# A four-layer image network on one core: image 0's gram matrix by transposes, weights made inside the loop, gram products of early images spread out

## The chip, the cores and the metric

The kernel runs on one NeuronCore of a Trainium2 chip. A core has four engines that compute: PE (matrix products, results in PSUM), DVE (vector work), ACT (activations and copies) and POOL. SP only issues DMAs; POOL issues some too. Each engine takes its own instructions in order and waits for others by semaphores; 16 DMA engines do the transfers. The metric is the time of one execution on the device, in microseconds (us), over three runs.

## The reference, cut to what matters

Sixteen images x of 64 channels and 128 x 128 points, in fp32, pass through four layers. Each layer is x + f(groupnorm(x)), with a norm over pairs of channels.

```
# layer 0
gram = einsum('bcn,bdn->bcd', xf, xf) / N          # xf = normed x, N = 128*128
f    = conv_w @ (gram @ xf)
# layer 1
f = |sobel_x(x)| + |sobel_y(x)|
# layer 2
f = conv3x3(temporal_shift(x), W) + b
# layer 3
y = conv1x1(conv3x3(x, w_bin), w1x1) + b1
f = clip(leaky(batchnorm(y)), 0, 255)              # batchnorm over all 16 images
```

Layer 0 needs the gram matrix of an image before anything else of that image can be computed, and the batch norm of layer 3 needs all images before anything can be written out.

## The kernel before

**What is set up.** Constants, biases and weights are loaded; the weights of layer 2 (w2, wm, pk2) and of layer 3 (w3, pk3, which are products of w_bin and w1x1, made by PE and copied by DVE) are put together at the start (lines 118 to 247). SP carries the constants, ACT's queue the weights. `consts` is one table `kc`; `k("I")`, its first 128 columns, is the identity.

**The loop.** The work is a list of steps written out by hand (line 911): 164 steps of four quarters q. Half an image, 64 rows, is 8 chunks of R = 8 rows; a tile has both halves of an image on its 128 partitions (64 channels twice). Front does layer 0's mixing and layer 1 (Sobel) for image b in the steps 15 + 8b to 22 + 8b, after a lead-in of three steps; Layer2 starts at 25 + 8b, Layer3 at 35 + 8b. Gram loads image b and makes its gram matrix ahead of Front. `InOrder` keeps each engine's instructions in the order in which this code issues them, so a place in the loop is a place in each engine's queue.

**Gram.** An image is read with its rows on partitions: eight loads `xr` of 8 channels each (three buffers), 512 KB in runs of 512 bytes, and eight ACT copies into `xw`, which holds for every row of the image its columns by channel, and a column of ones. Then 128 products `pg<-xw` (64 channels by 65) add up the gram matrix and the sums, in groups of 44, 42 and 42. `gram_chain` takes it to the mixing matrix `abd` and the coefficients `co` by small products, DVE operations and two square roots on ACT; each `yield` of it ends its turn in one quarter (`tick`). `pace` gives image b its first step and its speed: image 0 in steps 0 to 9 at one load per step and so on, with 4 steps for its chain; images 1 to 6 at double speed (2 units per quarter, four steps and a half); the later ones in eight steps and the chain. At double speed the three groups of products stand in three quarters one after the other.

**Front.** `load(i)` brings a chunk of x (two DMAs of 256 KB, two buffers). `mix(i, g)` multiplies half a chunk with `abd` into the PSUM tile `po` (one buffer); `prepare(i, g)` is ACT's normalization of it into `xh`; `sobel(i, q)` is six DVE operations, two absolute values on ACT, two more on DVE. The first of them, u<-xh with 1170 elements, starts a chunk and needs the chunk and one row of the next. At i = -3 Front also loads two edge rows (`xe`) and writes a row of zeros from `w0` to `x2_d`.

**The end.** As the last images finish, their results are read again with the layer's input, normalized and written out (lines 986 to 994).

Of the kernel before, what the change touches and what calls it, by code (L numbers as in the profile page):

```python
# [10 lines left out]
F32 = mybir.dt.float32  # L11
# [9 lines left out]
R = 8  # L21
# [23 lines left out]
def single(table, n):  # L45

    for o in range(2):
        planes = [i for m, i, half, _ in table if (m, half) == (n, o)]
        if len(planes) == 1:
            return o, planes[0]  # L50
# [58 lines left out]
def tile_kernel(ctx: ExitStack, tc: tile.TileContext, x, cw_h, w2_t, b2, wbin_t, w1_t, b1, gamma, beta, consts, out):  # L109
# [6 lines left out]
    small = ctx.enter_context(tc.tile_pool(name="small", bufs=4))  # L116

    kc = cpool.tile([P, K_END], F32, name="kc")
    nc.sync.dma_start(kc, consts)

    def k(name):
        return kc[:, AT[name][0]:AT[name][1]]

    def load_const(src, shape, name):
        t = cpool.tile(shape, F32, name=name)
        nc.sync.dma_start(t, src)
        return t

    cwh = load_const(cw_h, [P, C], "cwh")
    b2_sb = load_const(b2, [P, 1], "b2_sb")  # L130
    b1_sb = load_const(b1, [P, 1], "b1_sb")
    gamma_sb = load_const(gamma, [P, 1], "gamma_sb")
    beta_sb = load_const(beta, [P, 1], "beta_sb")
    bn_sum = cpool.tile([P, B * NS], F32, name="bn_sum")
    bn_sq = cpool.tile([P, B * NS], F32, name="bn_sq")

# [5 lines left out]
    def flat(ap):  # L142
        return ap.rearrange("p j w -> p (j w)")

    def halves(d, h, r0, n):

        v = d[0:C * HW].rearrange("(c r) -> c r", r=HW)
        return v[:, (h * HH + r0) * W:(h * HH + r0 + n) * W]
# [20 lines left out]
    def sv(name, n=1):  # L169
        return small.tile([P, n], F32, tag=name, name=name)  # L170

    def cols(o):
        return slice(o * C, (o + 1) * C)
# [13 lines left out]
    def sm(n, rows=P):  # L187
        if n > 8:
            return bank[0:rows, P:P + n]
        turn[0] = (turn[0] + 1) % 16  # L190
        return bank[0:rows, 8 * turn[0]:8 * turn[0] + n]
# [1 line left out]


    xw = wpool.tile([P, W // 2, C + 1, 2], F32, name="xw")
    nc.gpsimd.memset(xw[:, :, C, :], 1.0)

    xh = wpool.tile([P, 3, R + 2, W + 2], F32, name="xh")
    nc.gpsimd.memset(xh, 0.0)
    junk = wpool.tile([P, R * W], mybir.dt.bfloat16, name="junk")  # L200
    wbd = wpool.tile([P, P], F32, name="wbd")
    nc.gpsimd.memset(wbd, 0.0)

    w2 = wpool.tile([P, 3, 3, P], F32, name="w2")
    w3 = wpool.tile([P, 3, 3, P], F32, name="w3")
    nc.gpsimd.memset(w2, 0.0)
    nc.gpsimd.memset(w3, 0.0)
    for slot, i, o, ky in TO_SLOTS:
        nc.scalar.dma_start(w2[i * C:(i + 1) * C, slot, :, o * C:(o + 1) * C], w2_t[:, ky])

    wm = wpool.tile([P, 3, P], F32, name="wm")
    for n in range(2):
        o = 1 - single(TO_SLOTS, n)[0]
        nc.vector.tensor_copy(wm[:, :, cols(o)], w2[:, n, :, cols(o)])
    w0 = wpool.tile([P, P], F32, name="w0")
    nc.gpsimd.memset(w0, 0.0)

    wb = work.tile([P, R + 1, W + 2], F32, tag="u", name="wb")
    wb = flat(wb)[0:C, 0:9 * C].rearrange("p (y x c) -> p y x c", y=3, x=3)
    w1 = work.tile([P, R, W + 2], F32, tag="e", name="w1", bufs=1)[0:C, 0, 0:C]  # L220
    nc.scalar.dma_start(wb, wbin_t)
    nc.scalar.dma_start(w1, w1_t)
    for ky in range(3):
        pw = sm(3 * C, rows=C).rearrange("p (k c) -> p k c", k=3)
        for kx in range(3):
            nc.tensor.matmul(pw[:, kx, :], wb[:, ky, kx, :], w1, start=True, stop=True)
        for slot, i, o, kk in TO_PAIRS:
            if kk == ky:
                nc.vector.tensor_copy(w3[i * C:(i + 1) * C, slot, :, o * C:(o + 1) * C], pw)

    packed = {}
    for name, w, table in (("pk2", w2, TO_SLOTS), ("pk3", w3, TO_PAIRS)):
        nc.vector.tensor_add(w[:, 2], w[:, 0], w[:, 1])
        packed[name] = wpool.tile([P, 2, C], F32, name=name)
        for n in range(2):
            o, i = single(table, n)
            for kx, half in ((1, i), (0, 1 - i)):
                nc.vector.tensor_copy(
                    packed[name][half * C:(half + 1) * C, n], w[i * C:(i + 1) * C, n, kx, o * C:(o + 1) * C]
                )  # L240

    diffs, twins = {}, {}
    for name in ("d2", "d3"):
        diffs[name] = wpool.tile([P, 2, CP, W + 2], F32, name=name)
        nc.gpsimd.memset(diffs[name], 0.0)
        twins[name] = wpool.tile([P, 2, CP, W + 2], F32, name=f"q{name}")
        nc.gpsimd.memset(twins[name], 0.0)


    chains = []  # L250
# [50 lines left out]
    def gram_chain(b, pg):  # L301
# [77 lines left out]
            yield  # L379
        pk = sm(1)  # L380
        small_product(pk, pp.rearrange("p s c -> p (s c)"), k("q"))
        yield
        bias = sv("bias")
        dve.tensor_copy(bias, av[:, 2:3])
        st1 = sv("st1", 2)
# [18 lines left out]
        dve.tensor_copy(co[:, 3:4], mean)  # L404
        lead[b] = abd, co

    class Gram:
        first, last = 0, NS + 1

# [2 lines left out]

        def at(self, i, q):
            b = self.b
            CG = C // 8
            if i < NS:
                if q == 0 and i != 1:
                    for m in range(i + (1 if i == 2 else 2) if i else 0, min(i + 3, NS)):
                        t = xin.tile([P, CG, W], F32, tag="xr", name=f"xr_{b}_{m}", bufs=3)
                        sp.dma_start(t, x[b].rearrange("c h w -> h c w")[:, m * CG:(m + 1) * CG, :])  # L420
                        self.xr[m] = t

                if q == 3 and i > 0:
                    for m in (0, 1) if i == 1 else (i,):
                        act.copy(
                            xw[:, :, m * CG:(m + 1) * CG, :].rearrange("p w c t -> p c w t"),
                            self.xr.pop(m).rearrange("p c (w t) -> p c w t", t=2),
                        )
                return
            n = 4 * (i - NS) + q  # L430
            if n == 0:
                self.pg = ps_g.tile([P, CP, W], F32, tag="g", name=f"pg_{b}")[:, 0, 0:C + 1]

            for _ in range({0: 44, 2: 42, 4: 42}.get(n, 0)):
                w = self.w
                s = w % 2
                pe.matmul(
                    self.pg[s * C:(s + 1) * C, :], xw[:, w // 2, 0:C, s], xw[:, w // 2, :, s],
                    start=(w < 2), stop=(w >= W - 2),
                )  # L440
                last[0] = s
                self.w += 1
            if n == 6:
                chains.append(gram_chain(b, self.pg))


    lo, hi = slice(0, C), slice(C, P)
# [2 lines left out]
    class Front:  # L450
# [17 lines left out]
            self.xs[i] = t  # L468

        def mix(self, i, g):  # L470
            po = ps_po.tile([P, CP, W], F32, tag="po", name=f"po_{self.b}_{i}_{g}")
            small_product(po, self.abd, self.xs[i][:, g * CP:(g + 1) * CP, :])
            self.po[i, g] = po

# [8 lines left out]
        def at(self, i, q):  # L483
            b = self.b
            if q == 0:
                if i == -3:

                    self.xe = xin.tile([P, W], F32, tag="xe", name=f"xe_{b}", bufs=1)
                    sp.dma_start(self.xe[lo], x[b][:, HH, :])
                    sp.dma_start(self.xe[hi], x[b][:, HH - 1, :])  # L490
                    sp.dma_start(x2_d[b][0:W].rearrange("(p w) -> p w", p=1), w0[0:1, 0:W])
                if i + 3 < NS:
                    self.load(i + 3)
                if -1 <= i < NS - 1:
                    self.prepare(i + 1, 1)
                if 1 <= i:
                    self.store(i - 1)
                    act.activation(
                        junk.rearrange("p (j w) -> p j w", w=W), self.x2.pop(i - 1), AF.Square,
                        accum_out=self.st[:, 1, i - 1:i],  # L500
                    )
                if i == NS:
                    chains.append(coefficients(self.st, lambda co: coefs2.update({b: co}), b2_sb))
# [360 lines left out]
    def run(stage, b, i, q):  # L864
        if 0 <= b < B and stage.first <= i <= stage.last:
            if (stage, b) not in live:
                live[stage, b] = stage(b)
            live[stage, b].at(i, q)


    pace = {}
    at = 0
    for b in range(B):
        half = 1 <= b <= 2 * EARLY
        pace[b] = at, 2 if half else 1

        at += (NS // 2 if half else NS) + {0: 4, 2 * EARLY: 2}.get(b, 0)
    last_one = NS * (B - 1) + starts[0][1]
    steps = last_one + NS + 1

# [27 lines left out]
            loaded.append((yt, rt))  # L908
            fetched[0] += 1

    for step in range(steps):
        for q in range(4):
            for b in range(B):

# [8 lines left out]
            if q == 3:  # L923
                for b in range(B):
                    run(Layer2, b, step - starts[1][1] - NS * b, "last of 3")
            for b in range(B):
                at, n = pace[b]
                for m in range(n):
                    v = 4 * n * (step - at) + n * q + m
                    run(Gram, b, v // 4, v % 4)  # L930
            tick()

            if step == last_one - NS and q == 0:
# [99 lines left out]
```

## Time and profile before

| | us |
|---|---|
| median of 3 runs | 2804.1 (2804.09 to 2806.65) |
| profiled execution | 2800.37 |
| its span, first to last instruction | 2798.6 |
| PE / DVE / ACT / POOL busy | 2222.1 / 2201.4 / 2120.1 / 859.5 |
| gram products of image 0 (pg<-xw x256 records) | 26.7 to 36.7 |
| first mix (po<-x,abd) | 47.25 |
| first Sobel operation (step 15) | 59.08 |
| step 47 begins | 528.97 |

The span is that of the trace of one execution; the time of that execution includes what lies around it. "Busy" adds up the time in which an engine had an instruction running; a share of the whole span averages over stages with different limits, so a stage is read by itself. In the rows of the profile, "x256" counts records: an fp32 product leaves two. The number in brackets is the idle time of that engine before the row, and what ended it. Nearly all instructions have line 73, that of the helper which keeps order; they are told apart by their tiles, written output<-inputs.

Section 2 of the page, 40 equal slices of about 70 us, gives the tenths of busy time:

```profile
PE   4568899999999999999999999999999995000000
DVE  3999999898989898989898989999997435333332
ACT  4667779888888888888888888998997667333332
PEclk7679999999999999999999999999999998555555
```

Three regimes are seen: a ramp of some seven slices, a long middle with all engines near full, and an end in which PE has nothing to do and DMA writes the output.

### The profile page before, as it was taken

The numbers are of one execution on the slowest core, as the hardware profiler recorded it, in microseconds if no ns is written. First come the engines' busy times: TensorE is split into PE (matmuls) and PEld (weight loads), VectorE is DVE, ScalarE is ACT, GpSimd is POOL, SyncE is SP. The second block draws the span as 40 slices with busy tenths as digits, with TensorE's granted clock in tenths as the row PEclk, the third lists the DMA queues.
The fourth block names the chain that finished last, engine by engine and source line by source line (L and its number), as shares of the span: only waits on it lengthen the run. The fifth ranks groups of instructions, "written<-read, shape, count | busy, mean of one in ns | idle before, by whom it ended". The sixth has DMA issues, their size and how long they took to land. (4 is left out here: it accounts for less than half of the span.)

```text
span 2798.6 us, 46299 instructions
## 1 busy us (share of the span) xinstructions
PE 2222.1 (79%) x14772; PEld 1088.8 (39%) x14772; DVE 2201.4 (79%) x3758; ACT 2120.1 (76%) x3171; POOL 859.5 (31%) x1326
## 2 busy tenths in 40 slices
PE   4568899999999999999999999999999995000000
PEld 2323444444444545353534353566666641000000
DVE  3999999898989898989898989999997435333332
ACT  4667779888888888888888888998997667333332
POOL 1035433343434343434343434444444310000000
PEclk7679999999999999999999999999999998555555
DMA  6789878888888888888888777888877767999999
GB/s 168 196 221 233 237 198 237 218 232 212 230 215 221 222 220 219 222 216 227 221 219 227 214 184 197 209 204 214 209 207 187 218 192 273 420 420 420 420 420 387
DMA packets 688880, 685.95 MB, mean 245 GB/s; under 512 B 61744, under 2 KB 590144, under 8 KB 688640
## 3 DMA queue, kind: packets, MB, share of 16 engines
q1 hardware_dynamic: 662656, 614.42, 73.9%
q0 software_dynamic: 24576, 68.12, 10.0%
q8 instruction: 119, 1.95, 0.3%
q14 instruction: 121, 0.99, 0.1%
q10 hardware_dynamic: 1408, 0.46, 0.1%
HBM read 346.23 MB, written 268.44 MB: 220 GB/s over the span
## 5 line engine op out<-in xcount | busy, mean ns | idle before, releaser
L73 PE MATMUL two<-d,w 128*64 128x508 f32 (+2 forms) x2560 | 898.2, 586 | 0.0
L73 PE MATMUL two<-d,wi 128*64 128x508 f32 (+3 forms) x1536 | 626.6, 576 | 0.0
L73 POOL DMA_DIRECT2D qd<-d x512 | 269.8, 529 | 882.2 <-issue 330.0
L73 PE MATMUL two<-qd,pk 128*64 128x512 f32 (+1 forms) x1024 | 518.5, 587 | 1.6 <-DMA qd<-d 1.1
L73 POOL TENSOR_SCALAR edges<-v,co 64x8 f32<-64x8 f32 x512 | 335.2, 655 | 352.5 <-ACT v L73 244.4
L73 PE MATMUL po<-x,abd 128*64 128x512 f32 x1024 | 386.2, 631 | 60.4 <-ACT xh L73 60.4
L73 PEld LDWEIGHTS two<-d,w 128*64 128x64 f32 x2560 | 297.9, 136 | 288.7 <-issue 221.2
L73 PE MATMUL one<-v,w 128*64 128x508 f32 (+2 forms) x1600 | 409.0, 578 | 0.0
L73 PE MATMUL one<-v,wi 128*64 128x508 f32 (+3 forms) x1536 | 407.4, 590 | 0.0
L73 DVE TENSOR_TENSOR d<-v 128x512 f32<-128x512 f32 (+1 forms) x512 | 346.1, 679 | 44.4 <-POOL v L73 17.1
L73 ACT COPY qd<-d 64x512 f32<-64x512 f32 x512 | 315.2, 616 | 21.0 <-DVE d L73 14.5
L73 ACT ACTIVATE xh<-po,co 128x128 f32<-128x128 f32 (+1 forms) x480 | 275.3, 621 | 51.0 <-PE po L73 48.7
L73 DVE SCALAR_TENSOR_TENSOR e<-e 128x1032 f32<-128x1032 f32 (+1 forms) x256 | 313.2, 1223 | 0.0
L73 DVE SCALAR_TENSOR_TENSOR y<-two,c 128x1024 f32<-128x1024 f32 x128 | 156.1, 1219 | 125.6 <-ACT v L73 72.4
L73 PEld LDWEIGHTS two<-d,wi 128*64 128x64 f32 x1536 | 196.1, 135 | 143.2 <-issue 107.7
L73 POOL TENSOR_SCALAR v<-v,kc 128x9 f32<-128x9 f32 x256 | 238.4, 944 | 11.9
L73 ACT ACTIVATE v<-x,co 128x512 f32<-128x512 f32 (+2 forms) x368 | 234.9, 704 | 0.0
L73 PEld LDWEIGHTS one<-v,w 128*64 128x64 f32 x1600 | 163.3, 137 | 177.4 <-issue 130.0
L73 PEld LDWEIGHTS one<-v,wi 128*64 128x64 f32 x1536 | 156.0, 138 | 162.6 <-issue 126.4
L73 ACT ACTIVATE u<-u 128x1024 f32<-128x1024 f32 x128 | 135.4, 1058 | 90.3 <-DVE u L73 89.9
L73 DVE SCALAR_TENSOR_TENSOR u<-xh 128x1170 f32<-128x1170 f32 x128 | 175.7, 1372 | 12.2 <-ACT xh L73 9.8
L73 PEld LDWEIGHTS po<-x,abd 128*64 128x64 f32 x1024 | 111.0, 140 | 175.4 <-ACT xh L73 92.3
(154 smaller groups left out, 3442.4 us busy)
## 6 DMA issues: line engine op xcount, KB each, us to landing
xr<-in_x SPq DMA_DIRECT2D x128, 512.0 KB, 6.7
x<-in_x SPq DMA_DIRECT2D x256, 256.0 KB, 4.0
x_d<-u SPq DMA_DIRECT2D x512, 128.0 KB, 3.6
y_d<-y SPq DMA_DIRECT2D x512, 128.0 KB, 4.0
x_d<-x SPq DMA_DIRECT2D x496, 128.0 KB, 2.5
qd<-d POOLq DMA_DIRECT2D x256, 130.0 KB, 3.0
qd<-d POOLq DMA_DIRECT2D x256, 129.8 KB, 3.6
v<-x_d SPq DMA_DIRECT2D x448, 72.1 KB, 3.0
```

Source lines behind the costliest of these rows:

```text
L73: return self.tc.keep_in_program_order(call(*args, **kwargs))
```

## The change

Four things are done.

1. Image 0 leaves the class Gram. A new function `first_gram` runs ahead of the loop: it loads image 0 by channels in eight tiles (each two DMAs of 256 KB, runs of 4 KB), transposes 128 x 128 blocks of them on PE (64 in all) into PSUM, copies the two halves into `xw` on DVE and ACT, and makes the 128 gram products chunk by chunk, those of chunk m after the transposes of chunk m + 1. It then issues Front's lead-in for image 0 with the loads of two chunks, the eight loads of image 1 for its gram, and image 0's gram chain, with five of image 1's ACT copies between its links; the other three copies come in step 15. The loop starts at step 13.
2. The loads of constants and weights go to POOL's queue, but for the identity, which is first on SP. The products that make w3 move into steps 17, 18 and 19 (their copies to ACT), the rest of the weights into step 20 (copies on POOL, two additions on DVE).
3. Images 1 to 6 keep their steps, but each quarter has one unit of its own (`half(r)`): loads at r = 3 to 10, copies at 6 to 13, the groups of products at r = 14, 16 and 18 (image 1: one later), the chain from 19.
4. Two of the first mixes of image 0 use the PSUM buffers of `two` in place of `po`.

```diff
+    sp.dma_start(kc[:, 0:P], consts[:, 0:P])
+    pool.dma_start(kc[:, P:K_END], consts[:, P:K_END])
+    for t, src in ((wb, wbin_t), (w1, w1_t), (cwh, cw_h)):
+        pool.dma_start(t, src)
...
     for slot, i, o, ky in TO_SLOTS:
-        nc.scalar.dma_start(w2[i * C:(i + 1) * C, slot, :, o * C:(o + 1) * C], w2_t[:, ky])
+        pool.dma_start(w2[i * C:(i + 1) * C, slot, :, o * C:(o + 1) * C], w2_t[:, ky])
     w0 = wpool.tile([P, P], F32, name="w0")
+    pool.memset(w0, 0.0)
...
+    def weights_of_layer_3(ky):
+        pw = bank[C:P, 512 - 3 * C:512].rearrange("p (k c) -> p k c", k=3)
+        for kx in range(3):
+            pe.matmul(pw[:, kx, :], wb[:, ky, kx, :], w1, start=True, stop=True)
+        for slot, i, o, kk in TO_PAIRS:
+            if kk == ky:
+                act.copy(w3[i * C:(i + 1) * C, slot, :, o * C:(o + 1) * C], pw)
...
+    def first_gram():
+        pg = ps_g.tile([P, CP, W], F32, tag="g", name="pg_0")[:, 0, 0:C + 1]
+        src = []
+        t = sv("sd")
+        dve.memset(t, 1.0)
+        act.activation(t, t, AF.Sqrt)
+        for m in range(NS):
+            t = ring.tile([P, 2, CP, W], F32, tag="x3", name=f"x_first_{m}", bufs=NS + 2)
+            t = t.rearrange("p a j w -> p (a j w)")
+            for h in range(2):
+                sp.dma_start(t[h * C:(h + 1) * C], halves(x[0].rearrange("c h w -> (c h w)"), h, m * R, R))
+            src.append(t)
+        for m in range(NS + 1):
+            if m < NS:
+                two = ps_two.tile([P, 2, CP, W], F32, tag="two", name=f"turned_{m}").rearrange("p a j w -> p (a j) w")
+                for j in range(R):
+                    pe.transpose(two[:, j], src[m][:, j * P:(j + 1) * P], k("I"))
+                for h, copy in ((0, dve.tensor_copy), (1, act.copy)):
+                    copy(xw[:, m * R:(m + 1) * R, 0:C, h], two[:, :, h * C:(h + 1) * C])
+            if m > 0:
+                for w in range(2 * R * (m - 1), 2 * R * m):
+                    gram_product(pg, w)
+        run(Front, 0, Front.first, 0)
+        live[Front, 0].load(1)
+        for m in range(NS):
+            t = ring.tile([P, C // 8, W], F32, tag="x3", name=f"xr_1_{m}", bufs=NS + 2)
+            sp.dma_start(t, x[1].rearrange("c h w -> h c w")[:, m * C // 8:(m + 1) * C // 8, :])
+            rows.append(t)
+        for link, _ in enumerate(gram_chain(0, pg)):
+            if link in (2, 3, 4, 5, 6):
+                rows_to_columns(1, link - 2, rows[link - 2])
...
+        def half(self, r):
+            if self.b > 1 and 6 <= r < 6 + NS:
+                rows_to_columns(self.b, r - 6, self.xr.pop(r - 6))
+            if self.b > 1 and 3 <= r < 3 + NS:
+                self.load(r - 3)
+            self.part({14: 44, 16: 42, 18: 42}.get(r - (self.b == 1), 0))
+            if r - (self.b == 1) == 19:
+                chains.append(gram_chain(self.b, self.pg))
...
         def mix(self, i, g):
-            po = ps_po.tile([P, CP, W], F32, tag="po", name=f"po_{self.b}_{i}_{g}")
+            if self.b == 0 and (i, g) in ((0, 1), (1, 0)):
+                po = ps_two.tile([P, 2, CP, W], F32, tag="two", name=f"po_0_{i}_{g}")[:, 0]
+            else:
+                po = ps_po.tile([P, CP, W], F32, tag="po", name=f"po_{self.b}_{i}_{g}")
...
-    for step in range(steps):
+    for step in range(starts[2][1] - 2, steps):
...
+            first = starts[2][1]
+            if step == first and q < 3:
+                rows_to_columns(1, NS - 3 + q, rows[NS - 3 + q])
+            if q == 1 and first + 2 <= step < first + 5:
+                weights_of_layer_3(step - first - 2)
+            if q == 1 and step == first + 5:
+                other_weights()
```

More of the change, by code (lines that the diff above doesn't have):

```diff
@@ L118, in tile_kernel, with const @@
     kc = cpool.tile([P, K_END], F32, name="kc")
-    nc.sync.dma_start(kc, consts)
     def k(name):
         return kc[:, AT[name][0]:AT[name][1]]
[L124 to L133, printed above, removed]
+    def const(shape, name):
+        return cpool.tile(shape, F32, name=name)
+    cwh = const([P, C], "cwh")
+    b2_sb, b1_sb, gamma_sb, beta_sb = (const([P, 1], n) for n in ("b2_sb", "b1_sb", "gamma_sb", "beta_sb"))
     bn_sum = cpool.tile([P, B * NS], F32, name="bn_sum")
@@ L195, in tile_kernel @@
     xw = wpool.tile([P, W // 2, C + 1, 2], F32, name="xw")
-    nc.gpsimd.memset(xw[:, :, C, :], 1.0)
-    xh = wpool.tile([P, 3, R + 2, W + 2], F32, name="xh")
-    nc.gpsimd.memset(xh, 0.0)
+    pool.memset(xw[:, :, C, :], 1.0)
+    wb = ring.tile([P, (R + 1) * W + 2], F32, tag="v2", name="wb", bufs=3)
+    wb = wb[0:C, 0:9 * C].rearrange("p (y x c) -> p y x c", y=3, x=3)
+    w1 = ring.tile([P, R + 1, W], F32, tag="v3", name="w1")[0:C, 0, 0:C]
+    sp.dma_start(kc[:, 0:P], consts[:, 0:P])
+    pool.dma_start(kc[:, P:K_END], consts[:, P:K_END])
@@ L200, in tile_kernel @@
+    for t, src in ((wb, wbin_t), (w1, w1_t), (cwh, cw_h)):
+        pool.dma_start(t, src)
     junk = wpool.tile([P, R * W], mybir.dt.bfloat16, name="junk")
     wbd = wpool.tile([P, P], F32, name="wbd")
-    nc.gpsimd.memset(wbd, 0.0)
+    pool.memset(wbd, 0.0)
     w2 = wpool.tile([P, 3, 3, P], F32, name="w2")
     w3 = wpool.tile([P, 3, 3, P], F32, name="w3")
-    nc.gpsimd.memset(w2, 0.0)
-    nc.gpsimd.memset(w3, 0.0)
-    for slot, i, o, ky in TO_SLOTS:
-        nc.scalar.dma_start(w2[i * C:(i + 1) * C, slot, :, o * C:(o + 1) * C], w2_t[:, ky])
@@ L211, in tile_kernel @@
[L211 to L214, printed above, removed]
-    w0 = wpool.tile([P, P], F32, name="w0")
[L216 to L240, printed above, removed]
+    pool.memset(w3, 0.0)
@@ L242, in tile_kernel @@
+    xh = wpool.tile([P, 3, R + 2, W + 2], F32, name="xh")
+    pool.memset(xh, 0.0)
+    pool.memset(w2, 0.0)
+    for t, src in ((b2_sb, b2), (b1_sb, b1), (gamma_sb, gamma), (beta_sb, beta)):
+        pool.dma_start(t, src)
+    for slot, i, o, ky in TO_SLOTS:
+        pool.dma_start(w2[i * C:(i + 1) * C, slot, :, o * C:(o + 1) * C], w2_t[:, ky])
+    w0 = wpool.tile([P, P], F32, name="w0")
+    pool.memset(w0, 0.0)
     diffs, twins = {}, {}
@@ L244, in tile_kernel, with other_weights @@
         diffs[name] = wpool.tile([P, 2, CP, W + 2], F32, name=name)
-        nc.gpsimd.memset(diffs[name], 0.0)
+        pool.memset(diffs[name], 0.0)
         twins[name] = wpool.tile([P, 2, CP, W + 2], F32, name=f"q{name}")
-        nc.gpsimd.memset(twins[name], 0.0)
+        pool.memset(twins[name], 0.0)
+    def weights_of_layer_3(ky):
[5 more added lines that the diff above has]
+                act.copy(w3[i * C:(i + 1) * C, slot, :, o * C:(o + 1) * C], pw)
+    wm = wpool.tile([P, 3, P], F32, name="wm")
+    packed = {}
+    def other_weights():
+        for n in range(2):
+            o = 1 - single(TO_SLOTS, n)[0]
+            pool.tensor_copy(wm[:, :, cols(o)], w2[:, n, :, cols(o)])
+        for name, w, table in (("pk2", w2, TO_SLOTS), ("pk3", w3, TO_PAIRS)):
+            dve.tensor_add(w[:, 2], w[:, 0], w[:, 1])
+            packed[name] = wpool.tile([P, 2, C], F32, name=name)
+            for n in range(2):
+                o, i = single(table, n)
+                for kx, half in ((1, i), (0, 1 - i)):
+                    pool.tensor_copy(
+                        packed[name][half * C:(half + 1) * C, n], w[i * C:(i + 1) * C, n, kx, o * C:(o + 1) * C]
+                    )
     chains = []
@@ L381, in gram_chain @@
         small_product(pk, pp.rearrange("p s c -> p (s c)"), k("q"))
-        yield
+        if b > 1:
+            yield
         bias = sv("bias")
@@ L405, in gram_chain, with gram_product, rows_to_columns @@
         lead[b] = abd, co
+    def gram_product(pg, w):
+        s = w % 2
+        pe.matmul(
+            pg[s * C:(s + 1) * C, :], xw[:, w // 2, 0:C, s], xw[:, w // 2, :, s],
+            start=(w < 2), stop=(w >= W - 2),
+        )
+        last[0] = s
+    def rows_to_columns(b, m, t):
+        act.copy(
+            xw[:, :, m * C // 8:(m + 1) * C // 8, :].rearrange("p w c t -> p c w t"),
+            t.rearrange("p c (w t) -> p c w t", t=2),
+        )
+    rows = []
+    def first_gram():
[29 more added lines that the diff above has]
+                rows_to_columns(1, link - 2, rows[link - 2])
     class Gram:
@@ L414, in at @@
             b = self.b
-            CG = C // 8
             if i < NS:
@@ L418, in at @@
                     for m in range(i + (1 if i == 2 else 2) if i else 0, min(i + 3, NS)):
-                        t = xin.tile([P, CG, W], F32, tag="xr", name=f"xr_{b}_{m}", bufs=3)
-                        sp.dma_start(t, x[b].rearrange("c h w -> h c w")[:, m * CG:(m + 1) * CG, :])
-                        self.xr[m] = t
+                        self.load(m)
                 if q == 3 and i > 0:
                     for m in (0, 1) if i == 1 else (i,):
[L425 to L428, printed above, removed]
+                        rows_to_columns(b, m, self.xr.pop(m))
@@ L429, in at @@
                 return
             n = 4 * (i - NS) + q
[L431 to L442, printed above, removed]
+            self.part({0: 44, 2: 42, 4: 42}.get(n, 0))
@@ L443, in at, with part, load @@
             if n == 6:
                 chains.append(gram_chain(b, self.pg))
+        def part(self, n):
+            if self.w == 0 and n:
+                self.pg = ps_g.tile([P, CP, W], F32, tag="g", name=f"pg_{self.b}")[:, 0, 0:C + 1]
+            for _ in range(n):
+                gram_product(self.pg, self.w)
+                self.w += 1
+        def load(self, m):
+            t = xin.tile([P, C // 8, W], F32, tag="xr", name=f"xr_{self.b}_{m}", bufs=3)
+            sp.dma_start(t, x[self.b].rearrange("c h w -> h c w")[:, m * C // 8:(m + 1) * C // 8, :])
+            self.xr[m] = t
@@ L491, in at @@
                     sp.dma_start(x2_d[b][0:W].rearrange("(p w) -> p w", p=1), w0[0:1, 0:W])
-                if i + 3 < NS:
+                if i + 3 < NS and i + 3 not in self.xs:
                     self.load(i + 3)
@@ L868, in run @@
             live[stage, b].at(i, q)
+    first_gram()
     pace = {}
[L872 to L877, printed above, removed]
+    at = 12
+    for b in range(1, B):
+        pace[b] = at, 2 if b <= 2 * EARLY else 1
+        at += NS // pace[b][1] + (2 if b == 2 * EARLY else 0)
     last_one = NS * (B - 1) + starts[0][1]
@@ L925, in tile_kernel @@
                     run(Layer2, b, step - starts[1][1] - NS * b, "last of 3")
-            for b in range(B):
+            for b in range(1, B):
                 at, n = pace[b]
-                for m in range(n):
-                    v = 4 * n * (step - at) + n * q + m
-                    run(Gram, b, v // 4, v % 4)
+                if n == 1:
+                    run(Gram, b, step - at, q)
+                elif 0 <= step - at <= 5:
+                    live.setdefault((Gram, b), Gram(b)).half(4 * (step - at) + q)
+            first = starts[2][1]
[5 more added lines that the diff above has]
+                other_weights()
             tick()
```

## The prediction

> **What bounds the kernel now.** I read the page first: PE 79%, DVE 79% and ACT 76% of the span, and the chain of waits ends in the output pass, which is all DMA. None of that is touched. The change is at the head and in the ramp, so I cut the span by the start of each image block's first Sobel instruction on DVE (u<-xh, 128x1170), which comes once per step: 59.08 us for step 15, 528.97 for step 47, 1760.20 for step 119. From step 47 on every group of 8 steps takes 136.8 us and is full of PE work (windows below: 1220.22 of 1231.23 us). The loop has the same steps 15 to 163 afterwards, so whatever moves the first Sobel moves the end, and only steps 15 to 46 can add or give back.
>
> The windows view (busy us per engine, instructions, granted clock, DMA share, GB/s):
>
> ```profile
> 0.00:59.08 59.08, 22.98 (x330) 15.88 (x331) 14.17 (x64) 21.41 (x25) 9.79 (x15) 0.84 0.71 175
> 59.08:528.97 469.89, 392.93 (x3331) 181.42 (x3333) 442.35 (x809) 363.95 (x538) 171.07 (x234) 0.89 0.85 219
> 528.97:1760.20 1231.23, 1220.22 (x8196) 542.64 (x8193) 1142.88 (x2026) 1090.72 (x1703) 459.06 (x738) 1.00 0.82 217
> ```
>
> In the head no engine is busy half the time: it is latency. In the ramp DVE is the bound (442 of 470). The timeline of the head says which latency:
>
> ```profile
> 5.94 14.99 SPq L73 DMA_DIRECT2D xr<-in_x  x8
> ...
> 25.45 1.15 ACT L73 COPY xw<-xr 128x1024 f32<-128x1024 f32 x1 [0.70 <-DMA xr<-in_x]
> ...
> 26.74 9.93 PE L73 MATMUL pg<-xw 128*64 128x65 f32 x256 [14.69 <-ACT xw L73]
> ...
> 36.71 0.23 DVE L73 COPY gs<-pg 128x65 f32<-128x65 f32 x1 [20.69 <-PE pg L73]
> ...
> 47.62 0.20 ACT L73 ACTIVATE sd<-var 128x1 f32<-128x1 f32 x1 [8.46 <-DVE var L73]
> 47.73 3.20 ACT L73 COPY xw<-xr 128x1024 f32<-128x1024 f32 x3
> ...
> 52.61 1.98 PE L73 MATMUL po<-x,abd 128*64 128x512 f32 x4 [3.44 <-ACT xh L73]
> ...
> 59.08 1.38 DVE L73 SCALAR_TENSOR_TENSOR u<-xh 128x1170 f32<-128x1170 f32 x1 [9.84 <-ACT xh L73]
> ```
>
> Image 0 is loaded whole (to 25.5), then copied, and only then does the gram begin (26.7); it ends at **G = 36.7**. The small chain of products ends with its second square root at **S = 47.6**. ACT then makes three copies of image 1 before it may normalize, and mixes wait for the one po buffer; the first Sobel is at **F = 59.1**.
>
> **G, part by part.** Removed: small loads ahead of the image on SP (its first image load starts at 5.94) and the weight work of the head. Added: 64 transposes on PE, 16 copies of 512 elements. Loads: identity slice issued from 0.73, so the first x chunk's two halves go at about 1.1 and 1.7; x<-in_x lands 3.7 us after issue (median of the first 60 us), so PE starts at 5.4. The other chunks: 4.19 MB at 420 GB/s (the output pass, also 4 KB packets) to 268 GB/s (26.7 to 30.1 us, mixed with short packets): 10.0 to 15.6 us, last landing between 14 and 20.
>
> PE, per chunk, 8 transposes and 16 gram products. The gram rows of before run 62 records in 26.7:30.1 and 196 in 30.3:36.7; two records are one product: 108 ns each, then 65 ns once the granted clock rises. A transpose isn't in the trace. Nearest rows: bank<-w,wb with 64 moving columns takes one record per 107 ns at the start (the starts of the six records of a group), each record being half an fp32 product. A 128-column fp32 product at that clock is four of these, 0.427 us; if a transpose moves its data once, 0.107. Here the Trainium skill speaks both ways. "TensorE: Matmul & The Clock Gate", Part 4, gives 275 ns for a 128x128 transpose in a kernel and says that the full clock doesn't engage for transposes; its Terms call the transpose mode 4 times faster for fp32. I set the row against the 275 ns: the cold bank records last 311 ns each and still follow each other every 107, so 275 looks like a duration and not a pitch. I take **0.107 us**, and keep 0.054 and 0.427 as ends. By the page's pitch and cold products a chunk would be 8 x 0.275 + 16 x 0.108 = 3.93; by mine 2.58 cold and 0.86 + 1.04 = 1.90 warm. Three chunks cold and five warm are 17.2. The copies (DVE about 0.65 from the 64x192 copy at 350 ns and the 128x65 at 230; ACT 0.76 from xh<-po) lie beside PE in two PSUM buffers; only the last shows, 0.8. G = 5.4 + 17.2 + 0.8 = **23.4**. PE, not the loads, is late here.
>
> **S.** The chain itself is unchanged: 47.6 - 36.7 = 10.9, so S = 34.3 if nothing comes between. Five copies of image 1 now stand on ACT between its two square roots: 5 x 1.15 = 5.8 in a gap of 8.7, hidden if rows 0 to 4 have landed; if not, the second square root waits behind them. Their loads are behind the write of w0 on SP, which waits for w0's memset, late in POOL's queue: memsets 0.22 + 0.20 + 1.06 + 3.35 + 1.06, 14 DMA issues at 0.53 (qd<-d) = 7.4, so 14 us, or 22 if the w2 pieces cost double and more; I take 18. Then x chunks 0 and 1 and rows 0 to 4, 3.67 MB at 280 GB/s = 13.1, 2 for landing, 1.15 for the copy: 34.3. The two paths meet: **S = 34.5**, from 30 (no wait, fast loads) to 38.
>
> **F.** Before, F - S = 11.5. Afterwards ACT has no copies there (3.2 us gone), and three mixes run on PE without waiting for a buffer. At the low clock (0.50 in 47:59) a mix is 1.98: from S - 0.4 they end at S + 1.6, 3.6 and 5.5; the last normalization (0.76 + 0.36) follows: F = S + 6.6. What is late next is PE. So **F = 41.1, 18.0 earlier**.
>
> **The ramp, steps 15 to 46.**
> - Gram groups two quarters apart. In steps 16 and 20 PE has no gap (11.07 and 10.45 us) while DVE has 9.9 of work, so 1.2 and 0.6 are to be had; at 28 and 32 PE is full too (14.91 of 15.17, 13.92 of 13.92), DVE short by 1.7 and 0.7. Step 36 (20.34) is PE-full, but so are its neighbours: the group moves into step 35, nothing gained. Some are moved and not gained: -2, from 0 to -5.
> - Weights. Three small groups of products, six ACT copies of 0.35 to 0.45 in steps 17 to 19, where ACT has 3 to 5 us free per step; two DVE adds (0.55 each) in step 20, which DVE bounds: +1.1, and +0.4 for absolute values that ACT starts later. POOL's ten copies meet an idle POOL (0.2 us busy in step 20). +1.5, from 1 to 4.
> - Loads of images 2 to 6: per step 3, 3, 2, 0 become 1, 4, 3, 0; copies 2, 2, 2, 2 become 0, 2, 4, 2. A step with 4 loads, one x chunk and one store moves 3.1 MB, 11.7 us at 270 GB/s, against 12 to 15 us that such steps take now. 0, from -2 to +10: each copy has three quarters (7 to 9 us) for a landing of 5.7.
>
> Sum: -18.0 - 2 + 1.5 = -18.5. The profiled execution took 2800.37 (span 2798.6 and 1.8 around it), so 2781.9; the median of the runs is 3.7 above it, and I forecast **2785.6**.
>
> **Rivals.**
> - B, transposes at the page's price (275 ns, PE cold): 8 x 3.93 = 31.4, G = 37.6, S = 48.5, F = 55.1; 4.0 + 0.5 gained, 2799.6. For it: before the gram PE is idle, and the clock falls to 0.5 whenever work thins. Against: the 107 ns pitch.
> - C, loads take the gain back in the ramp: DMA share is 0.95 to 1.08 in steps 17, 21, 24, 25, 26, and ACT waits 11.8 us for xr there. Five images at 2 us: 2795.6. Against: the bytes are the same over four steps.
> - D, the other side: the fp32 transpose runs as four passes on a cold PE. Chunk 3.42 + 1.73 = 5.15, G = 47.4, F = 64.9, 5.8 later and 0.5 back in the ramp: 2809.4. If the weight loads of a whole-array product don't hide behind the one before, 0.85 each: G = 74.4, 2836.4. It decides from a pitch of 0.35 us (G = 42.1), and can be told from no change from 0.43. For it: every fp32 product in the trace costs that. Against: a transpose needs no arithmetic.
> - That the removed 13 steps were hidden anyway is excluded by DVE's 9.84 us idle at 59.08.
>
> **How the numbers follow.** Forecast (pitch up to 0.16; 2776 to 2792) 0.68; B 0.12; C 0.12; D 0.08. Low end: S = 30, F = S + 5.6, ramp -5, about 2775. High end: B, 2800. A measurement tells 0.2% (5.6 us) from none: faster is the forecast, C and part of B, 0.85; same, most of B, 0.08; slower, D, 0.07.
>
> **What will show it.** First Sobel near 41; gram's last product near 23; records with two<-x,kc at 0.107 us apart; the second square root right behind an ACT copy of xw, that one released by a DMA; steps 16, 20, 28 shorter, step 20's DVE longer by 1.1. Wrong if transposes are 0.3 us apart, if 15 to 47 takes over 475 us, or if step 47 on changes its 136.8.

## The result, and the profile after

The changed kernel takes **2794.4 us** (median of six runs, 2793.3 to 2795.0) against 2804.1 before (six runs, 2803.3 to 2808.3): ratio 0.9962, 95% interval 0.9949 to 0.9975. That is 9.7 us less, small but clear of noise. The forecast was 18.5 us less, 2785.6, so the gain is half of what the sum said. The time lies between the forecast's low end and its high end, 2775 and 2800, but above the 2776 to 2792 to which it gave most of its chance.

The profiled execution took 2793.3, its span is 2791.6, 7.0 less than the span before. The rest of the 9.7 is that the execution profiled before lay 3.7 us under its median, this one 1.1. The windows view, cut at the same places as before (first Sobel, step 47, step 119):

```profile
0.00:47.51 47.51, 30.55 (x378) 22.48 (x378) 12.87 (x55) 16.48 (x25) 19.50 (x35) 0.89 0.92 232
47.51:523.22 475.71, 395.38 (x3345) 189.34 (x3347) 443.30 (x812) 365.30 (x544) 169.61 (x238) 0.90 0.83 215
523.22:1754.59 1231.37, 1221.38 (x8201) 538.35 (x8199) 1142.64 (x2026) 1090.32 (x1703) 456.90 (x738) 1.00 0.83 217
```

The first Sobel is 11.6 us earlier (59.08 to 47.51); the ramp is 5.8 us longer (469.9 to 475.7), so half of that is given back; the middle is the same to 0.2 us. Each of these is one execution. The same head code gave a first Sobel at 59.1 and 62.1 in the two traces of the old head, and at 47.5, 48.0 and 49.0 in three of the new one, so single places in the head are known to 1.5 us at best. DMA share in the head rises from 0.71 to 0.92: the head is no longer latency alone. Its timeline:

```profile
9.37 3.96 PE L73 MATMUL turned<-kc,x_first 128*128 128x128 f32 x16 [9.37 <-DMA x_first<-in_x]
...
17.35 1.09 PE L73 MATMUL turned<-kc,x_first 128*128 128x128 f32 x8
...
18.37 1.23 PE L73 MATMUL pg<-xw 128*64 128x65 f32 x32
...
27.13 1.06 PE L73 MATMUL turned<-kc,x_first 128*128 128x128 f32 x8 [0.63 <-issue]
...
30.88 0.23 DVE L73 COPY gs<-pg 128x65 f32<-128x65 f32 x1 [1.95 <-PE pg L73]
...
38.90 1.15 ACT L73 COPY xw<-xr 128x1024 f32<-128x1024 f32 x1 [0.47 <-DMA xr<-in_x]
...
41.16 5.92 PE L73 MATMUL po<-x,abd 128*64 128x512 f32 x16
...
41.53 0.20 ACT L73 ACTIVATE sd<-var 128x1 f32<-128x1 f32 x1 [1.49 <-DVE var L73]
...
47.51 1.38 DVE L73 SCALAR_TENSOR_TENSOR u<-xh 128x1170 f32<-128x1170 f32 x1 [4.36 <-ACT xh L73]
```

PE's first transpose waits 9.4 us for data. The first two chunks of eight take 4 us together, one transpose every 0.213 us; later ones take 1.09, one every 0.109, beside 1.23 of gram products, 2.2 per chunk. (The granted clock in the profile reads 1.00 from 9.4 to 31 us, at both paces. "Low" and "full clock" are therefore read from the pace here, of which one is half the other.) The gram ends at 30.9, the second square root comes at 41.5 and was released by the chain (DVE var), not by the copies in front of it. The fifth of these copies, issued ahead of it, ended at 40.05, only 1.5 us earlier. The four mixes now run in one piece of 5.92 us.

The ramp by blocks of steps (us, from the start of one step's first Sobel operation to that of another), with the versions tried below:

| | first Sobel | steps 15-22 | 23-30 | 31 | 32-46 | 15-46 |
|---|---|---|---|---|---|---|
| before | 59.1 | 90.7 | 114.2 | 15.9 | 249.1 | 469.9 |
| changed | 47.5 | 89.7 | 114.8 | **21.5** | 249.6 | 475.7 |
| changed, old pace | 49.0 | 92.5 | 114.6 | 15.9 | 249.4 | 472.4 |
| before, new pace | 62.1 | 89.0 | 117.7 | 20.1 | 249.3 | 476.2 |
| late constants | 45.4 | 89.7 | 114.5 | 20.1 | 250.7 | 475.0 |
| and image 5 at old pace | 45.3 | 89.7 | 116.2 | 19.0 | 249.4 | 474.3 |
| and images 4 to 6 at old pace | 46.9 | 89.7 | 116.3 | 15.9 | 250.6 | 472.4 |
| all together | 44.7 | 89.7 | 115.8 | 15.9 | 249.4 | 470.9 |

One step carries nearly the whole loss. In step 31 of the kernel before, the waits view (waiter, releaser, us in total, times, longest) of ACT has no wait for a load of a later image (`xr`):

```profile
ACT v L73 <- DMA x_d<-x: 3.0, 1, 3.0
ACT u L73 <- DVE u L73: 0.9, 1, 0.9
ACT xh L73 <- PE po L73: 0.2, 1, 0.2
```

In the changed kernel ACT and then DVE have

```profile
ACT xw L73 <- DMA xr<-in_x: 7.7, 3, 3.9
...
DVE u L73 <- ACT u L73: 5.7, 1, 5.7
```

and SP's timeline shows why those loads are late. In the kernel before it has

```profile
259.47 7.22 SPq L73 DMA_DIRECT2D v<-x_d  x12
266.79 2.63 SPq L73 DMA_DIRECT2D x_d<-x  x4
269.52 0.56 SPq L73 DMA_DIRECT2D xr<-in_x  x1
```

and in the changed one

```profile
247.47 8.19 SPq L73 DMA_DIRECT2D v<-x_d  x12
255.75 0.39 SPq L73 DMA_DIRECT2D xr<-in_x  x1
256.24 3.02 SPq L73 DMA_DIRECT2D x_d<-x  x4
259.36 1.09 SPq L73 DMA_DIRECT2D xr<-in_x  x1
```

Two of image 5's loads now stand behind the twelve loads of layer 2's last chunk, one of them behind four stores too; before it was one load, at a place where ACT did not wait for it. ACT meets their copies in order, waits, and the absolute values behind the copies come 5.7 us late for DVE, which bounds the ramp.

### The profile page after: what moved, and what is told of

The parts are those of the page before. It is cut to its first block, busy times and chain, and to the rows that moved or that the text cites. A ratio compares the mean times of both kernels' runs of the same rounds, so it can differ in the third digit from the quotient of the medians.

```text
span 2791.6 us, 46444 instructions
## 1 busy us (share of the span) xinstructions
PE 2232.5 (80%) x14836; PEld 1097.1 (39%) x14836; DVE 2200.6 (79%) x3751; ACT 2115.3 (76%) x3177; POOL 865.2 (31%) x1350
## 3 DMA queue, kind: packets, MB, share of 16 engines
q8 instruction: 120, 1.97, 0.3%
## 5 line engine op out<-in xcount | busy, mean ns | idle before, releaser
L73 DVE TENSOR_TENSOR d<-v 128x512 f32<-128x512 f32 (+1 forms) x512 | 346.0, 679 | 41.5 <-POOL v L73 16.7
L73 PEld LDWEIGHTS two<-qd,pk 128*64 128x64 f32 x1024 | 128.6, 136 | 120.3 <-issue 81.2
```

The costliest lines, as they stand in the source:

```text
L73: return self.tc.keep_in_program_order(call(*args, **kwargs))
```

## The experiments

All but one were timed in several runs beside the kernel before on the same chip. The median of before in the four sets of runs was 2804.1, 2803.7, 2804.1 and 2801.6, so ratios are given where sets are compared. A ratio's interval is about 3.5 us wide on either side, and a difference of 2 us between two versions isn't clear of noise by times alone; there the traces carry the argument.

**The old pace for images 1 to 6, and the new pace alone.** The first is the changed kernel with the edit shown (image 1, which `first_gram` loads, keeps only its groups of products in the old places). The second is the kernel before with the new pace for images 2 to 6; its edit isn't shown.

```diff
-                elif 0 <= step - at <= 5:
-                    live.setdefault((Gram, b), Gram(b)).half(4 * (step - at) + q)
+                else:
+                    for m in range(2):
+                        v = 8 * (step - at) + 2 * q + m
+                        if b > 1 or v >= 4 * NS:
+                            run(Gram, b, v // 4, v % 4)
```

> The changed kernel, but images 1 to 6 keep the old pace: loads 3, 3, 2, 0 per step, two copies per step, three gram groups in neighbouring quarters. Theory (the new pace is what gives the gain back: in step 31 ACT waits 3.9 and 2.5 us for image 6's loads ahead of the absolute values, and DVE waits 5.7 us for those): step 31 takes 16 us as before and not 21.5, steps 15 to 46 take about 470 us and not 476, the first Sobel stays at 47.5, and the time is 3 to 6 us below the changed kernel's 2794.4, so 2788.5 to 2791.5. Rival (the stall in step 31 comes from elsewhere or is chance, and the new pace gains the 2 us that I forecast): 2794 to 2797.

> The kernel before, with the new pace for images 2 to 6 alone. Theory: 3 to 6 us slower than before, 2807 to 2810, with a long step somewhere in 17 to 33 in which ACT waits for an xr load. Rival: as forecast, about 2 us faster than before, 2802; steps 16 (image 1, old pace) as before, 20, 24, 28, 32 shorter.

With the old pace: 2792.5 (ratio 0.9959, 0.9947 to 0.9972), 2.0 under the changed kernel by medians, less than the 3 to 6 expected, and not told from it by the ratios. Step 31 is 15.9, the ramp 472.4 and not 470. ACT's waits in that step hold no xr load any more (the late loads are image 5's, not image 6's as I had written):

```profile
ACT v L73 <- DMA x_d<-x: 2.1, 1, 2.1
ACT u L73 <- DVE u L73: 1.2, 1, 1.2
ACT xh L73 <- PE po L73: 0.8, 1, 0.8
```

The new pace on the kernel before costs: 2807.6, ratio 1.0011 (1.0005 to 1.0018), 4.0 us beside the kernel before in the same set, and its step 31 takes 20.1. That the new pace loses time is shown by this run, and step 31 is long with it in every version that keeps it for all images. It does gain in steps 15 to 22, 2.7 us (89.7 against 92.5) in the changed kernel and 1.6 (89.0 against 90.7) in the kernel before.

**Weights twice.** What remains of the ramp with the old pace, 472.4 against 469.9 before, should be the weights.

```diff
+        for again in range(2):
             for kx in range(3):
                 pe.matmul(pw[:, kx, :], wb[:, ky, kx, :], w1, start=True, stop=True)
...
+                for again in range(2):
+                    other_weights()
```

> The changed kernel with the weights of layer 3 made twice in steps 17 to 19 and the rest twice in step 20. Theory (the weights in the loop cost the 2 us by which steps 15 to 46 of the version with the old pace are longer than before): 2 us more, 2796.4, most of it in step 20, where the DVE additions and what waits for POOL's copies stand. Rival (other engines' slack takes them, as for six of the twelve operations I forecast): under 0.7 us more.

2796.6, that is 2.2 more by medians, with ratios (0.9973, 0.9961 to 0.9984) whose intervals overlap. So making them in the loop costs some 2 us, an estimate from this doubling and from the difference of ramps (2.5), and not clear of noise. In the trace the added time is 1.7 in step 18, 1.1 in step 20 and 2.0 in step 28, where no weights are made (that step takes 14.0 to 17.2 in the versions tried, for no cause that was found); step 31 gets 1.9 back. Less of it was in step 20 than I expected.

**The upper halves from ACT's queue.**

```diff
-                sp.dma_start(t[h * C:(h + 1) * C], halves(...))
+                (sp, act)[h].dma_start(t[h * C:(h + 1) * C], halves(...))
```

> The changed kernel, the lower halves of image 0's chunks loaded from SP as before, the upper halves from ACT's queue, so that transfers into partitions 0 to 63 and into 64 to 127 are under way at the same time. Theory ([...]4 KB packets took 270 to 315 ns here and 159 in the output pass): image 0 has landed by 18 us and not 27.1, packets take near 160 ns, PE's 2.2 us per chunk is then the bound, the gram ends at 26 to 28 and not 30.9, time 2790 to 2792. Rival (two queues share what one had; the rate is that of the source): packets stay near 280 ns, last landing at 27, gram's end at 31, time 2794.

2794.3, no gain, but the edit brought a cost of its own: ACT issued its eighth load only at 13.6, when enough others had landed, and its copies of the transposed chunks stood behind, the first at 14.1 instead of 12.1. The gram ended at 32.8. At 10 to 14 us DMA moved 304 GB/s against 249 in the changed kernel, so the queues do matter somewhat, but the 420 of the output pass was not reached, and the theory isn't borne out. The first transpose came at 5.9 and not 9.4: the first chunk's two halves were issued at 0.9 and 1.2, both ahead of the constants on POOL's queue at 1.3. The next run bears on that.

**Late constants.**

```diff
-    pool.dma_start(kc[:, P:K_END], consts[:, P:K_END])
-    for t, src in ((wb, wbin_t), (w1, w1_t), (cwh, cw_h)):
-        pool.dma_start(t, src)
...
     pool.memset(w2, 0.0)
+    pool.dma_start(kc[:, P:K_END], consts[:, P:K_END])
+    for t, src in ((wb, wbin_t), (w1, w1_t), (cwh, cw_h)):
+        pool.dma_start(t, src)
```

> The changed kernel, POOL issues the constants (611 KB, 4380-byte packets) and w_bin, w1, conv_w after its memsets at 9 us, and not at 1.3. Theory (the first chunk lands at 9.4 because the constants share the transfer engines with it): first transpose at 5.5 to 6.5, and as PE then has the first chunks early but the bytes are the same, the last chunk lands at 26 to 27; the gram ends 1 to 3 us earlier and the time falls by as much, 2791.5 to 2793.5. Rival (the first landing is late because eight loads of 256 KB advance together): first transpose stays at 9, time 2794.

2792.2, 2.3 under the changed kernel by medians; but its runs spread from 2790.4 to 2797.8, and its ratio, 0.9961 (0.9948 to 0.9973), is that of the changed kernel. What the traces show is the head. The timeline of its head:

```profile
5.90 1.94 PE L73 MATMUL turned<-kc,x_first 128*128 128x128 f32 x8 [5.90 <-DMA x_first<-in_x]
...
16.73 1.06 PE L73 MATMUL turned<-kc,x_first 128*128 128x128 f32 x8 [1.59 <-DMA x_first<-in_x]
...
20.89 1.06 PE L73 MATMUL turned<-kc,x_first 128*128 128x128 f32 x8 [1.94 <-DMA x_first<-in_x]
...
29.11 0.23 DVE L73 COPY gs<-pg 128x65 f32<-128x65 f32 x1 [1.95 <-PE pg L73]
...
38.90 1.15 ACT L73 COPY xw<-xr 128x1024 f32<-128x1024 f32 x1 [0.36 <-DMA xr<-in_x]
39.94 0.19 ACT L73 ACTIVATE sd<-var 128x1 f32<-128x1 f32 x1
```

The first transpose comes 3.5 us earlier, the gram's end only 1.8: now PE waits for loads in the middle. And the second square root comes straight behind the fifth copy of image 1, which ends at 40.05 as in the changed kernel: the second path of the forecast's S is reached, and a still earlier gram would gain nothing without earlier loads of image 1.

**Each transpose twice.**

```diff
-                for j in range(R):
+                for j in (*range(R), *range(R)):
                     pe.transpose(two[:, j], src[m][:, j * P:(j + 1) * P], k("I"))
```

> The changed kernel with each of the 64 transposes made twice into the same place. Theory (from 9.4 to 26.5 us PE has no gap, so PE and not the loads sets the pace behind the first landing; a transpose takes 0.213 us at the low clock and 0.109 at the full one): 16 x 0.213 + 48 x 0.109 = 8.6 us more PE work, the last load no longer late, gram's end 7.5 to 8.6 us later, 38.5 to 39.5. Rival (loads set the pace, PE only follows): gram's end at most 2 us later. Beside it: 32 transposes in a row stand ahead of the first product, 6.8 us at the low clock; if transposes count as activity for the clock, their pitch falls to 0.109 before the first product; if they don't, all 32 stay at 0.213.

One run, 2799.9. The gram's end moved by 5.7 us, to 36.6, between the theory and the rival. The added transposes are 12 at 0.213 and 52 at 0.109, 8.2 us; the first 16 products now run at the full clock (0.8 saved), the 0.7 of waiting for the last load is gone, and it began 0.5 earlier. That leaves 6.2 for PE alone, near the 5.7 measured, so after the first landing PE sets the pace in the changed kernel. The other question has a clear answer:

```profile
8.89 6.64 PE L73 MATMUL turned<-kc,x_first 128*128 128x128 f32 x32 [8.89 <-DMA x_first<-in_x]
...
15.46 1.23 PE L73 MATMUL pg<-xw 128*64 128x65 f32 x32
16.61 1.97 PE L73 MATMUL turned<-kc,x_first 128*128 128x128 f32 x16
```

Of the first 32, which no product precedes, 28 follow each other at 0.213 us and the rest at 0.109, from 15.0 on; the next 16 take 1.97. Transposes do bring the full pace. With late constants it came 3.3 us after the first transpose and with no product before it; with two queues, where PE waited between the chunks, the transposes from 16.7 on were still at the low one. So it isn't a matter of the time since the start.

**Late constants and four loads from ACT.** The mended form of the two queues: only the first four upper halves go through ACT, which isn't held by them.

> Late constants as in the earlier run, and the upper halves of the first four chunks from ACT's queue (so that ACT isn't held by a full set of transfers in flight). Theory (transfers into both halves of the partitions at once are faster: 303 GB/s at 10 to 14 us in the earlier run with two queues against 256): chunks 1 to 3 land 1 to 2 us earlier than with late constants alone, gram ends at 27 to 28.5 and not 29.1, time 2790.5 to 2791.5. Rival (no gain, or ACT's issue time costs as much): 2792.

2791.8 (four runs), ratio 0.9954 (0.994 to 0.9967). The gram ended at 27.4, 1.7 earlier than with late constants alone (28.8 to 29.5 in three traces); the first Sobel came 0.6 earlier, which isn't told from chance. The medians of 2792.2 and 2791.8 don't tell them apart.

**Image 5 at the old pace, then images 4 to 6**, both with late constants; the condition of the first edit, with `b == 5` and with `b >= 4`.

> Late constants, and image 5 alone at the old pace. Theory (the long step 31 is one place: image 5's last two loads stand on SP behind the twelve v<-x_d loads of layer 2's last chunk and the four x_d<-x stores, and their copies on ACT one or two quarters ahead of absolute values; the new pace is worth 2 to 3 us everywhere else): step 31 at 16 us, steps 15 to 46 at 469 to 471, time 2786 to 2788. Rival (the stall moves to the next image's loads, or the new pace gains nothing elsewhere): 2790 to 2792.

> Late constants; images 1 to 3 keep the new pace, images 4 to 6 have the old one. Theory (with Front alone in the steps 15 to 22 the new pace gains 2.7 us over the old one, 89.7 against 92.5; from step 23 on, where layer 2's transfers share SP's queue, it gains nothing and loses step 31): steps 15 to 22 at 89.8, 23 to 30 at 114.6, step 31 at 16, steps 15 to 46 at 469 to 471, time 2786 to 2788. Rival (with an earlier start step 31 is long whatever the pace, as with image 5 alone at the old pace, where it took 19.0): step 31 at 19 to 21, time 2790.

Image 5 alone: 2790.3 (0.9946, 0.9933 to 0.996), and step 31 still 19.0. There ACT waited for layer 2's own last chunk:

```profile
ACT v L73 <- DMA x_d<-x: 7.4, 1, 7.4
```

On SP the same twelve loads were issued from 249.7 to 257.9 and those stores behind them. So my one place was too narrow. With images 4 to 6 at the old pace step 31 is 15.9 and the time 2789.2 (0.9948, 0.9934 to 0.9962); steps 23 to 30 came out 1.7 longer than expected, with step 28 at 16.6 as in several other versions. The times were 2.3 and 1.2 us above the upper end of what I had expected. That an earlier start makes step 31 long whatever the pace is refuted. Which of images 4 and 6 matters beside 5 wasn't tried.

**All together.** Images 4 to 6 at the old pace, late constants, four loads from ACT, and w2 and the small vectors held until the last chunk has been copied:

```diff
+        pool.tensor_copy(wm[:, 0, 0:1], xw[:, W // 2 - 1, 0, 0:1])
+        for t, source in ((b2_sb, b2), (b1_sb, b1), (gamma_sb, gamma), (beta_sb, beta)):
+            pool.dma_start(t, source)
+        for slot, i, o, ky in TO_SLOTS:
+            pool.dma_start(w2[...], w2_t[:, ky])
         run(Front, 0, Front.first, 0)
```

> The same, and the upper halves of the first four chunks from ACT's queue, and the loads of w2, the biases, gamma and beta held on POOL until the last chunk has been copied. Theory (these 0.3 MB in pieces of 256 bytes make the image's 4 KB packets slower, 313 ns and 213 GB/s at 16 to 18 us against 265 and 256 before): the last chunk lands at 21 to 22 and not 25, PE without a gap from its first transposes on, gram's end at 26 to 27, first Sobel at 42.5 to 44, time 1.5 to 2.5 us below the version before it in this call. Rival (PE is the bound already): gram's end at 27.4 as with two queues and late constants, no more than 1 us gained.

**2786.1**, ratio 0.9943 (0.993 to 0.9955), by medians 3.1 us under the version before it in the same set and the fastest of all, though the runs of the two overlap (2785.3 to 2789.1 and 2785.0 to 2790.5): some 15.5 us under before there. The gram's end, 28.2, is no better than the 27.4 of the mended two queues, so that the pieces of w2 slow the image down isn't shown; the first Sobel at 44.7 and a ramp of 470.9 make the time.

## Why the prediction was right, and where its size was off

**The direction and the mechanism held.** Steps 0 to 12 were latency; the first Sobel moved and took the end with it; steps 47 to 118 take 1231.4 us for 1231.2. For the chain from G to S it said 10.9, measured 10.7; from S to F 6.6, measured 6.0. But the first Sobel came 11.6 us earlier and not 18.0, and the ramp lost 5.8 where it was to gain 0.5. One of its signs of being wrong appeared: steps 15 to 46 took 475.7, over 475. That the time lies 1.2 us under rival C's number is chance: C put 10 us into the ramp and left the head as forecast. Five terms were mis-sized:

- **First landing, 5.4 forecast, 9.4 measured.** I took 3.7 us for a landing from rows of the head before. The constants that the change puts on POOL's queue share the engines: issued later they leave 5.9, with as many loads of the image queued, and two queues that got ahead of them gave 5.9 as well. "Removed: small loads ahead of the image on SP" was half true; they went to another queue and ran at the same time.
- **The transpose, 0.107 forecast, 0.213 at the low and 0.109 at the full clock measured.** The row was near, the reading one factor of two short: a transpose takes half of the 0.427 estimated for a product at the low clock, not a quarter. On the 16 cold ones that is 1.7 us. That 0.107 fits the warm ones is chance, for the row it came from was cold. The gram rows' change from 108 to 65 ns I put down to a rise of the granted clock; the windows view has 1.00 on both sides of it, so that clock doesn't show the change. Against the 275 ns of the Trainium skill ("TensorE: Matmul & The Clock Gate", Part 4): the records here last 273 ns and follow each other every 109, so 275 read as a pitch would have been wrong here.
- **Products and the last load.** A warm chunk took 2.2 and not 1.90, as its 16 products take 1.16 and not 1.04; the last load landed at 27.0, where I had 14 to 20. Together with the first two: 7.5 us on G, 30.9 for 23.4. Rival B's place (G at 37.6) wasn't reached, D's neither.
- **The second path into S, 34.3 forecast, 40.1 measured.** The fifth copy of image 1 ended at 40.05; SP issued these rows only from 27.1, when image 0's last chunk had landed. It stayed hidden by luck, because the gram was late too. With G at 23.4 and the same loads, S would still have been 40.1 and the first Sobel some 46 (an estimate: 40.1 and the measured 6.0), not 41.1.
- **The ramp, -0.5 forecast, +5.8 in the traces.** The step "loads of images 2 to 6 ... 0, from -2 to +10" is the one mis-sized: step 31 took 5.6 more. I set the bytes of four loads, one x chunk and one store against a step's length, and a landing against three quarters. The twelve loads of layer 2 and the four stores behind them on SP's queue were in neither sum. It is rival C's mechanism, in one step instead of five. The groups in themselves did what I said: step 16 lost 1.4 us (11.1 to 9.7). The weights were near, some 2 for 1.5.

At the level of times: head, weights and old pace 11.2 us under before in their set; the new pace takes 2.0 of it back by medians, and 4.0 on the kernel before.

## What to carry to other kernels

When a load is moved within a loop, count what is issued on its queue between its new place and its use, at the densest step and not on average; a copy on an in-order engine passes a late load on to everything behind it. When a head bound by latency is shortened, look at what the loads that were moved off its queue do on another one at the same time. And a duration in a profile isn't a pitch: take the distance of starts in a run of like instructions.

## What the runs showed that I had not expected

Transposes count as activity for TensorE's clock, as far as the pace tells: 28 of them at 0.213 us, then 0.109, before any product, while the profile's granted clock reads 1.00 throughout. The page named above says that the full clock doesn't engage for them; the measurement decides. And the image's 4 KB loads ran at 249 GB/s from 10 to 14 us and 217 from 14 to 18, with the engines' share above 1.0, where the output pass, of the same packet size and two thirds reads, has 420. Two queues brought 304 from 10 to 14; the cause stays open.
